# Reordering the prelude of a graph network kernel: edges loaded twice, a list made inside the scatter loop, and sixteen tiles taken up early

## The chip, the core and the metric

One core of a Trainium2 chip runs the whole kernel in one launch. The metric is the device time of one execution in microseconds (us). Engines are named as in the profile: PE (TensorE), PEld (its weight loads), DVE (VectorE), ACT (ScalarE), POOL (GpSimd) and SP (SyncE, which here only starts transfers).

## The reference

There are 6250 nodes of 256 features and 100,000 edges, sorted by destination. Two graph layers alternate with two mixtures of experts:

```python
edge_index = stack([src, dst])
x = x + L0_gnn(layernorm(x), edge_index, edge_weight)    # weighted, normed, self loops, two dense layers
x = x + L0_ffn(layernorm(x))                             # 8 experts, 2 taken
x = x + L1_gnn(edge_index, layernorm(x), edge_type_8)    # 8 relations
x = x + L1_ffn(layernorm(x))                             # 6 experts of three layers, 2 taken

# inside L0_gnn: rows are edge_index[0] (src), cols are edge_index[1] (dst)
deg  = segment_sum(edge_weight with 1 for self loops, row)
norm = rsqrt(deg)[row] * edge_weight * rsqrt(deg)[col]
xw   = x @ W
h    = segment_sum(xw[col] * norm[:, None], row) + b
out  = relu(h @ W1 + b1) @ W2 + b2
```

Layer 1 takes `hx[edge_type, src]` for each edge and sums it over `dst`.

## The kernel before, in words

Nodes are worked on in 49 blocks (`NT`) of 128. Edges come in 782 tiles (`C_`) of 128, and are padded to 784 (`TN`). Layer 0 turns every edge's product row into a message, which is scattered to a place in memory (`msgs`) where all messages of one source block lie together. A later stage sums them with matmuls. The stages that concern the change are these.

**The edges and the first branch (0 to about 49 us).** `e_dst`, `e_src`, `e_edge_type` and `e_edge_weight` are loaded as 125 partitions of 800. DVE counts for blocks 1 to 21 how many destinations lie below each block (`eqd`, L178), and ACT does so for blocks 22 to 48 (`sgd`, L183, a Sign with a running sum). Both fill `ltd`. POOL and DVE build four-word records (`rec`), which go to memory as `edge_table` and are read back by tile as `Mn` (128 partitions, 7 groups of 128 edges). A branch at L217 asks whether the edges need sorting. They don't.

**Layer 1's list (about 49 to 94 us).** From `Mn` come the lanes, the transposed `srcT` and `ewT`, and `lane_rows` in memory. `tile_list` then derives from `ltd` which edge tiles each destination block needs (`steps`, `past`, `natq_i`). Seven indirect gathers on POOL (L389) bring the tiles' records as `M`, from which `dlocT` and `idxT` are made for layer 1. Then the pool `edges` (`loading`, right side of the memory) is closed, and the next pool, `keys`, takes its room.

**Statistics, weights, block counts (about 50 to 143 us).** x is loaded by pairs of tiles (`xa`, L537) for the layer norm's mean and variance, and W is multiplied with W1 (`ww`). DVE compares each source block with 49 numbers (`eq`, L594), PE counts the result (`pcnt`), and a chain of small operations with a scan (L614) gives every block its start.

**Places and x@W (about 143 to 243 us).** For each of the 49 blocks, PE makes the places (`ppos`, L652 and L653), which DVE copies under a mask (L654). Between them the generator `x_times_w` loads x a second time and takes a tile at a time: ACT norms it (`xn`, L551), PE transposes it (`pt_x`), ACT copies it (`xT`), PE multiplies it (`pxw`, L562), ACT copies the product (L563), and SP writes it to `xw`.

**Degrees (about 243 to 372 us).** 28 chunks, each with a one-hot tensor (`ohl`, L722) and three weighted ones (`we`, L730) from DVE for PE's `pdeg` (L737).

**Scaling and scatter (about 372 to 1427 us).** `xw` is read back as `acc`, and ACT scales the 49 tiles by the degree's root (L775). A branch at L870 chooses between near and far edges; all are near. Its branch `messages` takes 98 turns of eight edge tiles. SP loads the turn's lanes three turns ahead (`rowsn`). DVE makes a selection `sT` (L823) and copies the sources into the message (L833). PE picks the rows (`pxn`, L842), ACT scales them by the edge weight (L857), and POOL scatters them with one indirect transfer per edge tile (L860).

The program is written with pools of tiles and generators. A scheduler decides the order of instructions on each engine, so it can differ from the order of the text. Each engine then works its own queue in order.

Of the kernel before, what the change touches and what calls it, by code (L numbers as in the profile page):

```python
# [8 lines left out]
F32 = mybir.dt.float32  # L9
I32 = mybir.dt.int32  # L10
# [32 lines left out]
RW = 260  # L43
DCH = 28
# [12 lines left out]
def gnn_ffn_kernel(ctx: ExitStack, tc: tile.TileContext, a, out):  # L57
# [20 lines left out]
    gap = graph_a.enter_context(tc.tile_pool(name="graph_a", bufs=1))  # L78
    loading = ctx.enter_context(ExitStack())
# [11 lines left out]
    src = load_edges("src", I32)  # L91
    et = load_edges("edge_type_8", I32)
    ew = load_edges("edge_weight", F32)
# [62 lines left out]

    table = dram.tile([C_, 128 * 4], I32, name="edge_table")  # L160
    records = table.rearrange("c (e r) -> (c e) r", r=4)
    rec = sp.tile([EP, EC, 4], I32, name="rec")
    recf = rec.bitcast(F32)
    hi_i = sp.tile([EP, EC], I32, name="hi_i")
    nc.vector.tensor_scalar(hi_i, dst, 7, None, op0=OP.arith_shift_right)
    hi = sp.tile([EP, EC], BF16, name="hi")
    nc.vector.tensor_copy(hi, hi_i)


    ltd = sp.tile([EP, NT + 1], F32, name="ltd")  # L170
    nc.vector.memset(ltd[:, 0:1], 0.0)
    nc.vector.memset(ltd[:, NT:], float(EC))
    edge = sp.tile([128, NT], F32, name="edge")
    nc.vector.tensor_scalar(edge, lanes_i[:, :NT], -1.0, 0.5, op0=OP.mult, op1=OP.add)
    by_count = 22
    for b in range(1, by_count):
        eqd = sp.tile([EP, EC], BF16, name=f"eqd{b}", tag="eqd")
        nc.vector.tensor_scalar(  # L178
            eqd, hi, float(b), None, op0=OP.is_lt, op1=OP.add, accum_out=ltd[:, b : b + 1]
        )  # L180
    for b in range(by_count, NT):
        sgd = sp.tile([EP, EC], BF16, name=f"sgd{b}", tag="sgd")
        nc.scalar.activation(  # L183
            sgd, hi, AF.Sign, bias=edge[:EP, b : b + 1], accum_out=ltd[:, b : b + 1]
        )
    nc.vector.tensor_scalar(
        ltd[:, by_count:NT], ltd[:, by_count:NT], -0.5, float(EC // 2), op0=OP.mult, op1=OP.add
    )
    nc.gpsimd.tensor_copy(rec[:, :, 0], dst)
    nc.gpsimd.tensor_copy(rec[:, :, 1], src)  # L190
    nc.gpsimd.tensor_copy(recf[:, :, 2], ew)
    nc.vector.scalar_tensor_tensor(rec[:, :, 3], src, float(NR), et, op0=OP.mult, op1=OP.add)
    nc.sync.dma_start(records[:E].rearrange("(p c) r -> p (c r)", p=EP), rec)
    pad = sp.tile([C_ * 128 - E, 4], I32, name="pad")
    nc.vector.memset(pad, 0)
    nc.vector.memset(pad[:, 0:1], NP + 128)
    nc.sync.dma_start(records[E:], pad)

    falls = sp.tile([EP, 2], F32, name="falls")
    fall = sp.tile([EP, EC], BF16, name="fall")  # L200
    nc.vector.tensor_tensor(fall[:, : EC - 1], hi[:, 1:], hi[:, : EC - 1], OP.is_lt)
    nc.vector.tensor_reduce(falls[:, 0:1], fall[:, : EC - 1], axis=AX.X, op=OP.max)
    nhi_i = sp.tile([EP, 1], I32, name="nhi_i")
    nc.vector.tensor_scalar(nhi_i, dnext, 7, None, op0=OP.arith_shift_right)
    nhi = sp.tile([EP, 1], BF16, name="nhi")
    nc.vector.tensor_copy(nhi, nhi_i)
    nc.vector.tensor_tensor(falls[:, 1:2], nhi, hi[:, EC - 1 :], OP.is_lt)
    pfall = psum_sm("pfall")
    nc.tensor.matmul(pfall[:1, :2], ones[:EP, 0:1], falls, start=True, stop=True)
    nfall = sp.tile([1, 1], F32, name="nfall")  # L210
    nc.vector.tensor_reduce(nfall, pfall[:1, :2], axis=AX.X, op=OP.max)
    nfall_i = sp.tile([1, 1], I32, name="nfall_i")
    nc.vector.tensor_copy(nfall_i, nfall)
    unsorted = nc.values_load(
        nfall_i[0:1, 0:1], min_val=0, max_val=EP, skip_runtime_bounds_check_because="it is a count"
    )
    with tc.If(unsorted > 0):  # L217
        with tc.tile_pool(name="reorder", bufs=1) as rp:
            cntd = rp.tile([EP, NT], F32, name="cntd")
            nc.vector.tensor_sub(cntd, ltd[:, 1:], ltd[:, :NT])  # L220
            ptot = psum_sm("ptotd")
            nc.tensor.matmul(ptot[:EP, :NT], ones[:EP, :EP], cntd, start=True, stop=True)
            ppre = psum_sm("ppred")
            nc.tensor.matmul(ppre[:EP, :NT], before[:EP, :EP], cntd, start=True, stop=True)
            tot = rp.tile([EP, NT], F32, name="totd")
            nc.vector.tensor_copy(tot, ptot[:EP, :NT])
            base = rp.tile([EP, NT], F32, name="based")
            nc.vector.tensor_tensor_scan(base, ones[:EP, :NT], tot, -1.0, op0=OP.mult, op1=OP.add)
            nc.vector.tensor_sub(base, base, tot)
            nc.vector.tensor_add(base, base, ppre[:EP, :NT])  # L230
            pos = rp.tile([EP, EC], F32, name="posd")
            one = ones[:EP, 0:1].to_broadcast([EP, EC])
            eq = rp.tile([EP, EC], BF16, name="eqd2")
            run = rp.tile([EP, EC], F32, name="rund")
            for b in range(NT):
                nc.vector.tensor_scalar(eq, hi, float(b), None, op0=OP.is_equal)
                nc.vector.tensor_tensor_scan(run, one, eq, base[:, b : b + 1], op0=OP.mult, op1=OP.add)
                nc.vector.copy_predicated(pos, eq.bitcast(U16), run)
            pos_i = rp.tile([EP, EC], I32, name="posd_i")
            nc.vector.tensor_copy(pos_i, pos)  # L240
            for c in range(EC):
                ins = nc.gpsimd.indirect_dma_start(
                    out=records,
                    out_offset=bass.IndirectOffsetOnAxis(ap=pos_i[:, c : c + 1], axis=0),
                    in_=rec[:, c, :],
                    in_offset=None,
                )
                tc.declare_no_dep(ins.ins, group="reorder", reason="every edge has a place of its own")
                tc.add_to_no_dep_group("reorder", ins.ins)

    def tile_list(s, pool, e0, e1, turns):

        def col1(name, dt=F32):
            return pool.tile([NT, 1], dt, name=f"{name}{s}", tag=f"tl_{name}")

        some = col1("some")  # L260
        nc.vector.tensor_tensor(some, e1, e0, OP.is_gt)
        e0_i, e1_i = col1("e0", I32), col1("e1", I32)
        nc.vector.tensor_copy(e0_i, e0)
        nc.vector.tensor_scalar(e1_i, e1, 127.0, None, op0=OP.add)
        nc.vector.tensor_scalar(e0_i, e0_i, 7, None, op0=OP.arith_shift_right)
        nc.vector.tensor_scalar(e1_i, e1_i, 7, None, op0=OP.arith_shift_right)
        f, nt = col1("f"), col1("nt")
        nc.vector.tensor_copy(f, e0_i)
        nc.vector.tensor_sub(nt, e1_i, e0_i)
        nc.vector.tensor_mul(nt, nt, some)  # L270
        pt0 = psum_sm(f"pt0_{s}")
        nc.tensor.matmul(pt0[:NT, 0:1], before[:NT, :NT], nt, start=True, stop=True)
        tend, ahead = col1("tend"), col1("ahead")
        nc.vector.tensor_add(tend, pt0[:NT, 0:1], nt)
        nc.vector.tensor_sub(ahead, f, pt0[:NT, 0:1])
        psh = psum_sm(f"psh_{s}")
        nc.tensor.matmul(psh[:NT, 0:1], nextup[:NT, :NT], ahead, start=True, stop=True)
        steps = pool.tile([NT, 2], F32, name=f"steps{s}", tag="tl_steps")
        nc.vector.memset(steps, 1.0)
        nc.vector.tensor_copy(steps[:, 1:2], psh[:NT, 0:1])  # L280
        past = pool.tile([NT, turns], F32, name=f"past{s}", tag="t4")
        nc.vector.tensor_scalar(past, turn[:NT, :turns], tend, None, op0=OP.is_ge)
        return steps, past, tend

    Mn = sp.tile([128, QN, 128, 4], I32, name="Mn")
    nc.vector.memset(Mn[:, QN - 1], NP + 128)
    whole = (QN - 1) * 128
    nc.sync.dma_start(  # L290
        Mn[:, : QN - 1].rearrange("p q e r -> p q (e r)"), table[:whole].rearrange("(q p) x -> p q x", p=128)
    )
    nc.sync.dma_start(Mn[: C_ - whole, QN - 1].rearrange("p e r -> p (e r)"), table[whole:])
    Mnf = Mn.bitcast(F32)
    firstb_i = sp.tile([128, QN], I32, name="firstb_i")
    nc.vector.tensor_scalar(firstb_i, Mn[:, :, 0, 0], 7, None, op0=OP.arith_shift_right)
# [447 lines left out]
    for _ in xws:  # L744
        pass
# [916 lines left out]
```

## Time and profile before

| what | us |
|---|---|
| the three runs | 4180.68, 4183.84, 4184.01 |
| their median | 4183.84 |
| the profiled execution | 4184.38 |
| its span in the trace | 4182.6 |
| first message scatter starts | 400.7 |
| last message scatter | about 1427 |

The profile has one execution of the program. Its time is 1.8 us longer than the span of its records. Rows of groups give busy time and mean duration, and then the time that the engine stood idle ahead of them, with what ended that idle time. A row of a stretch of time gives the busy time of each engine in it.

### The profile page before, as it was taken

The page shows a single profiled execution, that of the slowest core. Times are in us where ns is not written, and L with a number is a line of the kernel's source. Part 1 is how long each engine was busy: PE and PEld are TensorE (multiplying, and loading weights), DVE is VectorE, ACT ScalarE, POOL GpSimd, SP SyncE. Part 2 cuts the span into 40 slices and gives each one's busy share as a digit, 9 for nine tenths or more (in the row PEclk, how much of TensorE's full clock was granted, in tenths as well). Part 3 has the DMA queues.
Part 4 walks back from the last instruction along what each step waited for, and adds up shares of the span by engine and source line. Part 5 has one row for each costly group of instructions (what it writes and reads, how often), then busy time and mean ns, then how long its engine had stood idle before and what let it go on. Part 6 is the DMA issues. An engine that isn't in the chain of part 4 may idle for free.

```text
span 4182.6 us, 53223 instructions
## 1 busy us (share of the span) xinstructions
PE 3478.2 (83%) x14645; PEld 2313.5 (55%) x14645; DVE 2083.1 (50%) x5720; ACT 1310.2 (31%) x2934; POOL 2261.2 (54%) x2440
## 2 busy tenths in 40 slices
PE   2887777777777568888969967998679999999999
PEld 1565656655656345555547733444356666666656
DVE  6686211111111146777853367664456666666652
ACT  3312333333333212333324434665012222222213
POOL 1001777777777524555550057333767777777750
PEclk8998999999999788999989988999689999999999
DMA  5514433333333434555643335445645555555540
GB/s 178 170 38 148 131 128 127 128 128 127 127 127 128 159 102 158 191 201 188 214 165 108 109 122 199 196 196 201 187 140 152 151 153 153 147 154 153 146 115 9
DMA packets 233067, 612.09 MB, mean 146 GB/s; under 512 B 41908, under 2 KB 126103, under 8 KB 212783
## 3 DMA queue, kind: packets, MB, share of 16 engines
q0 software_dynamic: 100624, 294.88, 22.7%
q1 hardware_dynamic: 112636, 290.21, 20.8%
q10 hardware_dynamic: 19488, 23.31, 1.6%
q8 instruction: 132, 2.16, 0.2%
q14 instruction: 187, 1.53, 0.1%
HBM read 371.49 MB, written 236.79 MB: 145 GB/s over the span
## 4 chain that ended last, share of the span: by engine, by line
PE 41%; DVE 12%; DMA 5%; issue 5%; POOL 2%; ACT 2%; DVEq 1%; ACTq 0%; SPq 0%; POOLq 0%
PE ph_e1a L475 6%; PE py1a L1007 6%; PE pa1a L928 6%; PE ph_e2a L475 5%; PE pa0e L901 4%; PE phx L1425 4%; DMA g0e<-msgs 3%; DVE acc L903 3%; PE pf L1344 2%; PE pf L1360 2%; DVE rest L1435 1%; DVE acc L932 1%; PE pt_fh L463 1%; DVE hx L1419 1%; PE pg2e L1094 1%
## 5 line engine op out<-in xcount | busy, mean ns | idle before, releaser
L860 POOL DMA_INDIRECT msgs<-msgn,at x782 | 787.4, 1007 | 550.3 <-DMA M<-edge_table,natq_i 313.6
L920 POOL DMA_INDIRECT g1a<-hx,idxT x830 | 828.6, 998 | 319.1 <-PE pa1a L928 142.5
L842 PE MATMUL pxn<-acc,sTn 128*128 x3128 | 792.2, 413 | 242.1 <-DVE sTn L823 215.3
L842 PEld LDWEIGHTS pxn<-acc,sTn 128*128 128x128 f32 x3128 | 613.9, 206 | 420.3 <-DVE sTn L823 282.2
L901 PE MATMUL pa0e<-g0e,m0e 128*128 128x256 f32 x1660 | 503.3, 436 | 157.5 <-DVE acc L903 71.8
L857 ACT ACTIVATE msgn<-pxn,ewT 128x256 f32<-128x256 f32 x782 | 370.1, 473 | 638.5 <-PE pxn L842 468.0
L932 DVE TENSOR_TENSOR acc<-acc,pa1a 128x256 f32 x830 | 346.7, 418 | 341.8 <-PE pa1a L928 309.8
L901 PEld LDWEIGHTS pa0e<-g0e,m0e 128*128 128x128 f32 x1660 | 293.0, 207 | 330.6 <-issue 128.5
L898 POOL TENSOR_SCALAR m0e<-minus,keye 128x128 f32<-128x128 f32 x414 | 259.5, 641 | 320.0 <-PE pa0e L901 275.7
L833 DVE COPY msgn<-srcT 128x32 f32<-128x32 f32 x98 | 17.5, 181 | 831.1 <-DMA msgs<-msgn,at 722.1
L928 PE MATMUL pa1a<-g1a,m1a 128*128 128x256 bf16 x2490 | 375.6, 283 | 51.6 <-DMA g1a<-hx,idxT 35.0
L928 PEld LDWEIGHTS <-m1a 128*128 128x128 bf16 x2490 | 244.0, 100 | 275.2 <-issue 192.3
L903 DVE TENSOR_TENSOR acc<-acc,pa0e 128x256 f32 x830 | 347.2, 418 | 92.7 <-PE pa0e L901 42.9
L1425 PE MATMUL phx<-wr,xT 128*128 128x512 f32 x784 | 368.5, 613 | 29.1 <-DVE rest L1435 21.6
L1007 PE MATMUL py1a<-w_L_ffn_expert_w,v2a 128*128 128x256 f32 x1176 | 286.6, 384 | 6.0 <-DVE acc L932 3.0
L475 PE MATMUL ph_e1a<-xT3a,w_L_ffn_expert_w 128*128 128x512 f32 (+2 forms) x672 | 287.9, 555 | 0.0
L475 PE MATMUL ph_e2a<-v1a,w_L_ffn_expert_w 128*128 128x512 f32 (+2 forms) x672 | 280.1, 542 | 2.1 <-DVE acc L932 1.3
L482 ACT ACTIVATE v1a<-ph_e1a,cols 128x512 f32<-128x512 f32 (+2 forms) x168 | 106.5, 634 | 538.8 <-PE ph_e1a L475 525.7
L1425 PEld LDWEIGHTS phx<-wr,xT 128*128 128x128 f32 x784 | 148.2, 197 | 188.5 <-issue 161.2
L1385 POOL DMA_INDIRECT y<-ys,ats x98 | 97.5, 995 | 277.5 <-issue 262.2
L1007 PEld LDWEIGHTS py1a<-w_L_ffn_expert_w,v2a 128*128 128x128 f32 x1176 | 208.8, 190 | 44.2 <-ACT v2a L482 10.3
L1008 DVE SCALAR_TENSOR_TENSOR X<-py1a,C1a,X 128x256 f32<-128x256 f32 x294 | 138.9, 480 | 112.3 <-PE py1a L1007 111.4
(646 smaller groups left out, 4373.2 us busy)
## 6 DMA issues: line engine op xcount, KB each, us to landing
g0e<-msgs SPq DMA_DIRECT2D x104, 1040.0 KB
hx<-hx SPq DMA_DIRECT2D x49, 1536.0 KB
rowsn<-lane_rows SPq DMA_DIRECT2D x98, 256.0 KB
fx<-xs SPq DMA_DIRECT2D x105, 128.0 KB
ys<-fy ACTq DMA_DIRECT2D x105, 128.0 KB
g1a<-hx,idxT POOLq DMA_INDIRECT x830, 3.1
msgs<-msgn,at POOLq DMA_INDIRECT x782, 2.4
msgs<-none ACTq DMA_DIRECT2D x10, 650.0 KB
```

The lines of the kernel that those rows point to most:

```text
L475: nc.tensor.matmul(ps[:, :ncols], w[:, k, f * 128 : (f + 1) * 128], xT[:, k, :ncols], start=(k == 0), stop=(k == 1),)
L842: nc.tensor.matmul(come, sT[:, k, j, :], acc[:, bass.ds(blocks[j] * D + k * D, D)], start=(k == 0), stop=(k == 1),)
L857: nc.scalar.activation(msg[:, j, :D], come, AF.Copy, scale=ewT[:, t0 + j : t0 + j + 1])
L860: ins = nc.gpsimd.indirect_dma_start(out=msgs, out_offset=bass.IndirectOffsetOnAxis(ap=at[:, t0 + j : t0 + j + 1], axis=0), in_=msg[:, j, ...
L898: nc.gpsimd.tensor_scalar(m[:, j], minus, key[:, j : j + 1], None, op0=OP.is_equal)
L901: nc.tensor.matmul(ps[:, :D], m[:, j, :], g[:, j, :D], start=True, stop=True)
L903: nc.vector.tensor_add(here, here, ps[:, :D])
L920: nc.gpsimd.indirect_dma_start(out=g, out_offset=None, in_=table, in_offset=bass.IndirectOffsetOnAxis(ap=idxT[:, t0 + j : t0 + j + 1], axi ...
L928: nc.tensor.matmul(ps[:, :D], m[:, j, :], g[:, k * D : (k + 1) * D], start=(k == 0), stop=(k == 2))
L932: nc.vector.tensor_add(here, here, ps[:, :D])
L1007: nc.tensor.matmul(ps[:, :D], hT[:, k, j : j + 128], w[:, k, :], start=(k == 0), stop=(k == 1))
L1425: nc.tensor.matmul(ps, xT[:, k, :], wr[:, k, r : r + 2, :].rearrange("p r o -> p (r o)"), start=(k == 0), stop=(k == 1),)
```

## The change

The changed kernel takes up the work ahead of the scatter in another order.

- The three edge arrays that are needed by tile are loaded from the inputs in that form too (`dst_n`, `src_n`, `ew_n`). `edge_table` is still written, now by POOL's queue, and is not read back as a whole unless the edges have to be sorted.
- The first 16 tiles of x are loaded on ACT's queue and stay in memory (`x1`). Their statistics and norms come before the first branch, and their products with `ww` before the pool `edges` is closed. The norms' root is taken on DVE by `inverse_root`, not with ACT's square root.
- All 48 counts of destinations are on ACT, and stand in the text ahead of the degrees. DVE's part of the counts is gone, save in the branch that sorts.
- Layer 1's list, and the block lists of layer 0's sums, are made by a generator `lists`. From the eleventh turn of the scatter loop on, each turn takes one step of it. The seven gathers take one buffer `M` in turn.
- The lanes are loaded two turns ahead, not three.
- The scaling of `acc` is split: odd tiles on DVE, even ones on ACT.

```diff
+X1 = 16
...
-    src = load_edges("src", I32)
-    et = load_edges("edge_type_8", I32)
-    ew = load_edges("edge_weight", F32)
+    def load_tiles(name, dt, fill):
+        t = sp.tile([128, QN, 128], dt, name=f"n_{name}")
+        nc.vector.memset(t[:, QN - 1], fill)
+        e0, e1 = (QN - 1) * 128 * 128, E // 128 * 128
+        nc.sync.dma_start(
+            t[:, : QN - 1], a[name][:e0].rearrange("(q p e) -> p q e", p=128, e=128)
+        )
...
+    dst_n = load_tiles("dst", I32, NP + 128)
+    src_n = load_tiles("src", I32, 0)
+    ew_n = load_tiles("edge_weight", F32, 0.0)
+    x1 = sp.tile([128, X1, D], F32, name="x1")
+    for t in range(0, X1, 4):
+        nc.scalar.dma_start(
+            x1[:, t : t + 4], a["x"][t * 128 : (t + 4) * 128].rearrange("(t p) d -> p t d", p=128)
+        )
...
+    src = load_edges("src", I32)
+    et = load_edges("edge_type_8", I32)
+    ew = load_edges("edge_weight", F32)
...
-    by_count = 22
-    for b in range(1, by_count):
-        eqd = sp.tile([EP, EC], BF16, name=f"eqd{b}", tag="eqd")
-        nc.vector.tensor_scalar(
-            eqd, hi, float(b), None, op0=OP.is_lt, op1=OP.add, accum_out=ltd[:, b : b + 1]
-        )
-    for b in range(by_count, NT):
-        sgd = sp.tile([EP, EC], BF16, name=f"sgd{b}", tag="sgd")
-        nc.scalar.activation(
-            sgd, hi, AF.Sign, bias=edge[:EP, b : b + 1], accum_out=ltd[:, b : b + 1]
-        )
...
-    nc.vector.scalar_tensor_tensor(rec[:, :, 3], src, float(NR), et, op0=OP.mult, op1=OP.add)
-    nc.sync.dma_start(records[:E].rearrange("(p c) r -> p (c r)", p=EP), rec)
+    row8 = sp.tile([EP, EC], I32, name="row8")
+    nc.gpsimd.tensor_scalar(row8, src, float(NR), None, op0=OP.mult)
+    nc.gpsimd.tensor_tensor(rec[:, :, 3], row8, et, OP.add)
+    nc.gpsimd.dma_start(records[:E].rearrange("(p c) r -> p (c r)", p=EP), rec)
...
+    for t in range(X1):
+        x_stats(t, x1[:, t])
+    x_norms(0, X1)
+    multiply_weights()
     unsorted = nc.values_load(
...
-    nc.sync.dma_start(
-        Mn[:, : QN - 1].rearrange("p q e r -> p q (e r)"), table[:whole].rearrange("(q p) x -> p q x", p=128)
-    )
...
-    nc.vector.tensor_scalar(real, Mn[:, :, :, 0], float(NP), None, op0=OP.is_lt)
+    nc.vector.tensor_scalar(real, dst_n, float(NP), None, op0=OP.is_lt)
...
-    nc.sync.dma_start(lane_rows.rearrange("(q p) e -> p q e", p=128), laneb)
+    nc.gpsimd.dma_start(lane_rows.rearrange("(q p) e -> p q e", p=128), laneb)
...
-    steps, past, tend = tile_list("d", sp, bounds[:, 0:1], bounds[:, 1:2], Q * 128)
...
-    M = sp.tile([128, Q, 128, 4], I32, name="M")
-    for q in range(Q):
-        nc.gpsimd.indirect_dma_start(
...
-    dlocT = to_edges("dlocT", ed, Q, lambda q: dloc[:, q], BF16)
-    idxT = to_edges("idxT", ed, Q, lambda q: idxf[:, q], I32)
+    xws1 = x_times_w([(t, 2) for t in range(0, X1, 2)], x1)
+    for _ in xws1:
+        pass
     loading.close()
...
+    pairs = [(t, min(2, NT - t)) for t in range(X1, NT, 2)]
+    for t, n in pairs:
+        x = x_tiles(t, n, "a")
+        for i in range(n):
+            x_stats(t + i, x[:, i])
+    x_norms(X1, NT)
+    xws = x_times_w(pairs)
...
+    for b in range(1, NT):
+        sgd = kp.tile([EP, EC], BF16, name=f"sgd{b}", tag="sgd")
+        nc.scalar.activation(sgd, hi, AF.Sign, bias=edge[:EP, b : b + 1], accum_out=ltd[:, b : b + 1])
...
-        nc.scalar.activation(here, here, AF.Copy, scale=dinv[:, t : t + 1])
+        if t % 2:
+            nc.vector.tensor_scalar(here, here, dinv[:, t : t + 1], None, op0=OP.mult)
+        else:
+            nc.scalar.activation(here, here, AF.Copy, scale=dinv[:, t : t + 1])
...
+    def lists(pool, tag):
...
+        for q in range(Q):
+            M = pool.tile([128, 128, 4], I32, name=f"M{tag}{q}", tag="M")
+            nc.gpsimd.indirect_dma_start(
+                out=M.rearrange("p e r -> p (e r)"),
+                out_offset=None,
+                in_=table,
+                in_offset=bass.IndirectOffsetOnAxis(ap=natq_i[:, q : q + 1], axis=0),
+            )
+            yield
+            both = pool.tile([128, 2, 128], F32, name=f"both{tag}{q}", tag="both")
+            nc.vector.tensor_scalar(both[:, 0], M[:, :, 0], first[:, q : q + 1], None, op0=OP.subtract)
+            nc.vector.tensor_copy(both[:, 1], M[:, :, 3])
+            yield
...
-        with tc.tile_pool(name=f"expand{tag}", bufs=3) as xp:
+        with tc.tile_pool(name=f"expand{tag}", bufs=2) as xp, tc.tile_pool(name=f"lists{tag}", bufs=1) as lp:
...
-            ahead = [lanes_of(t0) for t0 in (0, 8, 16)]
+            ahead = [lanes_of(t0) for t0 in (0, 8)]
+            later = lists(lp, tag)
...
-                if t0 + 24 < TN:
-                    ahead.append(lanes_of(t0 + 24))
+                if t0 + 16 < TN:
+                    ahead.append(lanes_of(t0 + 16))
+                if t0 >= 80:
+                    next(later, None)
```

## The prediction

> **What bounds the kernel now.** I read the page's slices first, then busy time by stage, then groups of instructions in the first 401 us, then branches and waits. The change reaches two places only: the prelude, up to the first message scatter at 400.7 us, and the scatter itself, up to about 1427 us. The other 2756 us keep their instructions, so I cost them at nothing.
>
> ```profile
> DVE  6686211111111146777853367664456666666652
> ACT  3312333333333212333324434665012222222213
> POOL 1001777777777524555550057333767777777750
> PEclk8998999999999788999989988999689999999999
> ...
> L860 POOL DMA_INDIRECT msgs<-msgn,at x782 | 787.4, 1007 | 550.3 <-DMA M<-edge_table,natq_i 313.6
> L833 DVE COPY msgn<-srcT 128x32 f32<-128x32 f32 x98 | 17.5, 181 | 831.1 <-DMA msgs<-msgn,at 722.1
> ```
>
> A digit is a 104.6 us slice. In the scatter (slices 5 to 13) POOL shows 7, DVE 1. POOL issues 782 scatters in (1427 - 400.7) = 1026 us, 1.31 us each, 1.007 of them busy. DVE idles 722 us there for message buffers. So POOL bounds the scatter, and small DVE, PE or ACT work is free there; POOL instructions are not.
>
> The prelude has no single bound. Busy time by stage:
>
> ```profile
> 0.00:50.00 50.00, 0.50 (x3) 0.27 (x3) 31.72 (x80) 29.75 (x55) 8.11 (x14) 1.00 0.29 103
> 50.00:100.00 50.00, 22.81 (x94) 15.14 (x95) 28.34 (x110) 10.10 (x21) 7.97 (x9) 0.63 0.76 259
> 100.00:143.00 43.00, 27.23 (x122) 15.25 (x122) 37.61 (x134) 6.54 (x15) 0.00 (x0) 0.78 0.36 101
> 143.00:243.00 100.00, 94.63 (x479) 65.71 (x478) 53.59 (x101) 52.81 (x136) 0.00 (x0) 0.97 0.56 175
> 243.00:372.00 129.00, 112.46 (x788) 92.50 (x786) 121.34 (x121) 0.37 (x1) 0.00 (x0) 0.95 0.01 4
> 372.00:401.00 29.00, 3.56 (x8) 2.87 (x9) 5.51 (x19) 20.58 (x51) 0.28 (x1) 0.53 0.97 311
> ```
>
> After the stretch and its length come PE, PEld, DVE, ACT, POOL, granted clock, DMA share, GB/s. To 50 us DVE and ACT count edges; to 143 everything waits in turn; to 243 PE is full (places and x@W); to 372 DVE is full (degrees) and ACT empty; to 401 ACT scales.
>
> ```profile
> L183 ACT ACTIVATE sgd<-hi,edge 125x800 bf16<-125x800 bf16 x27 | 26.0, 961 | 17.3 <-DVE edge L174 16.4
> L537 DVE BATCH_NORM_STATS2 st<-xa 128x6 f32<-128x256 f32 x49 | 19.1, 409 | 10.5 <-DMA xa<-in_x 10.4
> L594 DVE TENSOR_SCALAR eq<-hib 128x784 bf16<-128x784 bf16 x49 | 14.3, 350 | 0.0
> L654 DVE COPY_PREDICATED pos<-eq,ppos 128x392 f32<-128x392 uint16 x98 | 52.5, 587 | 44.4 <-PE ppos L653 44.3
> L551 ACT ACTIVATE xn<-xb,shift,ln_o 128x256 f32<-128x256 f32 x49 | 26.9, 601 | 2.9 <-DVE shift L543 2.9
> L775 ACT ACTIVATE acc<-acc,deg_o 128x256 f32<-128x256 f32 x49 | 19.9, 493 | 4.3 <-DMA acc<-xw 4.3
> ```
> ```profile
> 133.15 2.07 PE L562 MATMUL pxw<-ww,xT 128*128 128x256 f32 x4
> ...
> 149.26 1.03 PE L562 MATMUL pxw<-ww,xT 128*128 128x256 f32 x4
> ```
> ```profile
> L870 DVEq COMPARE_BRANCH  x1: 72/72/72, 375.1 to 375.1; - x1
> L870 SPq COMPARE_BRANCH  x1: 50/50/50, 385.3 to 385.3; - x1
> ```
>
> **The change part by part**, along the chain of stages.
>
> *To the first branch.* DVE passes L217 at 48.5 us in before, after waiting 11.5 us for ACT's 27 counts. Gone from DVE: 21 counts (20.6 + 1.7 us), that wait, and the record product (1.6). Added: statistics of 16 tiles, 16 x (0.39 + 0.17) = 9 us, and a dozen small operations, 2 to 3 us. DVE is then limited by arrival: edges twice (2.8 MB), x1 (2.1 MB). At the 259 GB/s of the second stretch 4.9 MB take 19 us, and land at about 25; statistics and norms end near 36 (30 to 42). POOL's own additions (row product and sum about 4 us beside copies of 2.0, 2.0, 1.6) end near 29, an estimate from those copies, ahead of it. x1's four issues take at most 6 us of ACT (five fillers took 7.3 later), which idles 16 us there; the nine tile loads share SP's queue with the later edge loads, and only POOL's copies wait for those; the table and lane writes now on POOL's queue meet a POOL idle until the scatter, and only gathers 600 us later read the table: nothing each. The table write (1.6 MB, 17.3 to 33.1 us in before, the read-back's end) is no longer waited for here. **-12.5** (-7 to -18.5). The Trainium skill, "DMA: Bandwidth & Descriptors", section "Issuing engines are not separate DMA queues", speaks against this part: transfers issued by different engines run on the same 16 DMA engines, so moving x1 to ACT's queue buys issue time, not bandwidth. The row shows a share of only 0.29 in the first 50 us, so there is room; by the rule with the 103 GB/s of that row, 4.9 MB would take 48 us and all this gain would be gone. I take 259, since the small figure is mostly idle.
>
> *Branch to the free edge pool.* In before, layer 1's list (seven gathers, landing 4.2 us each, its small chain, 62.6 to 93.9 us) holds the right-hand pool; the next stage starts at 93.6. In after the list is gone, but the pool holds x1, and the next stage waits for the last x1 tile to be normed. That is a new serial chain. srcT and ewT come about 6 us behind the branch as now (42), then eight pairs. Pair time warm: PE 2 x (0.60 transposes + 1.03 products) = 3.3, with hand-overs 3.6; cold 2 x (1.06 + 2.07) = 6.3 by the first line at 133 us. The Trainium skill, "TensorE: Matmul & The Clock Gate", section "Part 1: The HAM clock gate", says that an idle window of about 3.4 us halves the clock. The granted clock in this stretch is 0.63, so both happen. Warm, the last norm comes at 42 + 7.5 x 3.6 = 69; cold at 42 + 7.5 x 6.3 = 89. Because PE has continuous work here, I take 69 (64 to 80). The pool's free point moves from 93.6 to 69: -24.6, of which 12.5 are counted above, so **-12**. DVE meanwhile does the other 33 tiles' statistics (18.5 us), which fit the 33 us from branch to 69.
>
> *Equality and counts of blocks.* 93.6 to 127.1 in before, 33.5 us: 49 eq (14.3), statistics between, and waits for xa. With the statistics gone ahead, 14.3 + 3 = 17.2. **-16**.
>
> *To the first predicated copy.* 15.9 us in before (127.1 to 143.0). ACT's counts are now 48, at 0.96 + 0.19 less overlap = 1.087 each. The diff puts them beside the degrees, where ACT is empty; the schedule puts 15 of them, 16.3 us, ahead of ACT's copy of the block counts, on which scan and places wait. With the norms of the remaining tiles and three xn between, the copy comes 20.3 us into this step, then 8.5 us of scan chain: 28.8. **+13** (0 to +17; had the schedule followed the text it were 0).
>
> *Places and x@W.* 100.3 us in before, PE-bound at 4.07 per two blocks. In after 33 tiles remain and each two carry two counts: ACT 1.10 + 0.65 + 0.72 + 2.17 = 4.65, so ACT becomes the bound: 16.5 x 4.65 = 77, minus 9 already done in the gap before, plus the last 16 blocks at DVE's 1.07 = 17. 84 to 85. **-16** (-8 to -22).
>
> *Degrees.* DVE-bound, same instructions: 0. Cover for the counts if they ran here: 129 us of idle ACT.
>
> *Scaling and the branch.* 49 scales at 0.406 on ACT become 25 there and 24 on DVE; alone -2, because the last loaded piece lands no earlier than 394.1 on the old clock. But DVE, which passed L870 at 375.1 and had 6.3 us of jump hidden, now passes it behind the last piece, near 395.5; then message copies, first list operations (0.64) and the first sT (1.47). SP and POOL are already past. The first scatter comes 6 us later after the end of the degrees: **+6** (0 to +8).
>
> *Scatter.* Seven gathers on POOL at 1.28, an iota 0.2, and the second gather two scatters behind the first, into the same buffer: its landing and two DVE operations less two scatters leave a stall of 1.5. **+10.7** (+9 to +20). Hidden: about 35 small PE, 14 DVE and ACT operations, under DVE's 722 us of waiting; without this cover about 15 us. The lanes' loads, three ahead before and two now, land 5.9 us after issue and have two turns, 21 us.
>
> Sum: -12.5 - 12 - 16 + 13 - 16 + 6 + 10.7 = **-27**. Against the profiled execution's 4184.4 (span 4182.6) that is 4157; the median, 4183.8, is 0.5 lower, which I ignore.
>
> **The rivals.**
>
> A. *More than that.* The norms wait less and x1 arrives early (branch at 31, pool free at 62), the second gather doesn't stall and DVE's jump costs 2: -27 - 7 - 4 - 2 = -40: 4144. For it: ACT and DMA have idle room everywhere. Against: each step must go well.
>
> B. *Cold TensorE.* The pair chain runs at 6.3, the pool is free at 89 to 92: -27 + 22 = -5: 4179, no change that can be told. For it: PEclk 0.63 and the two product lines. Against: in this stretch PE idled behind DVE and gathers, which go.
>
> C. *Slower: the pool is held still longer.* x1's chain is the one thing that holds it now. If PE and ACT alternate without overlap on a cold clock, a pair takes 6.3 + 2.5 (ACT's 2 x (0.55 + 0.33 + 0.36)) = 8.8: free at 42 + 7.5 x 8.8 = 108, 39 later: +12: 4196. It decides from (8.4 + 27)/7.5 = 4.7 us beyond 3.6, so 8.3 a pair. For it: each tile goes ACT, PE, ACT, PE, ACT. Against: three xn buffers and two pairs of output let the tiles overlap, as they do after 149 us.
>
> D. *It doesn't do what it says*: the counts really hide under the degrees, none ahead of the copy: -40, which joins A; or they are all in front: 33 more x 1.087, of which the places stage gives back most: about -18, inside my range.
>
> **How the numbers follow.** About 0.2% (8.4 us) can be told from no change. Chances: forecast 0.60 (4146 to 4172), A and the good side of D 0.17, B 0.13, C 0.10. Range: 4137 (A and a little) to 4183 (B whole), leaving out most of C and the far end of A. Faster: 0.60 + 0.17 = 0.77, same 0.13, slower 0.10.
>
> **What would show it.** Right: the first branch on DVE near 36; products in x1's chain at 1.03 per tile; the first block equality near 69; ACT counts ahead of the copy; pair cycle 4.65; first scatter near 363; scatter stage 1037 us with seven gathers. Wrong: the first equality beyond 90 (B, C), a scatter stage beyond 1046, or any longer stage after it. Outside the first 1400 us there should be no difference over 3 us.

## The result

The changed kernel took 4165.88 us (median of 5 runs, 4165.19 to 4166.91), the kernel before 4183.84 in the same set. The ratio is 0.9956 (95% interval 0.9943 to 0.9969): 18 us faster, where 27 were forecast. The profiled span went from 4182.6 to 4164.9 us, 17.7 less. A second set on another chip gave 4171.28 against 4182.07, ratio 0.9969 (0.9959 to 0.9980), so the gain is 11 to 18 us by the two medians.

The slices of the changed kernel's page and its rows for the scatter and the message copies:

```profile
DVE  4596111111111146787853367664556666666652
ACT  2802433333333212333324434665012222222113
POOL 1002777777777525555550057333777777777750
...
L919 POOL DMA_INDIRECT msgs<-msgn,at x782 | 785.2, 1004 | 271.2 <-DMA msgs<-msgn,at 128.6
L892 DVE COPY msgn<-srcT 128x32 f32<-128x32 f32 x98 | 17.8, 184 | 825.8 <-DMA msgs<-msgn,at 730.9
```

DVE's first slice fell from 6 to 4, ACT's second rose from 3 to 8: that is where most of the counts went. The scatter reads as before, POOL at 7 and DVE waiting 731 us for message buffers. Busy time by stage, with the changed kernel's own boundaries (stretch and length, then PE, PEld, DVE, ACT, POOL, clock, DMA share, GB/s):

```profile
0.00:52.00 52.00, 7.35 (x31) 5.45 (x31) 19.09 (x91) 7.09 (x14) 13.77 (x20) 0.94 0.76 226
52.00:88.00 36.00, 24.99 (x113) 18.77 (x114) 17.75 (x67) 15.99 (x42) 0.99 (x1) 0.81 0.68 227
...
135.00:217.00 82.00, 74.48 (x375) 48.81 (x374) 50.81 (x101) 60.81 (x148) 0.00 (x0) 0.98 0.53 168
```

In the first 52 us every engine is mostly idle (DVE busy for 19 us, POOL 14, ACT 7), while the DMA share is 0.76; in the first 50 us of the kernel before it was 0.29. The places (135 to 217) are still PE's: 74.5 of 82.

The steps by the starts of the instructions that bound them, in us:

| step | before | after | difference | forecast |
|---|---|---|---|---|
| start to DVE's first branch | 48.5 | 51.6 | +3.1 | -12.5 |
| branch to the free edge pool (`srcT_i`) | 45.1 | 36.8 | -8.3 | -12 |
| to the last equality | 33.1 | 18.2 | -14.9 | -16 |
| to the first predicated copy | 16.3 | 28.2 | +11.9 | +13 |
| places, to the last copy | 99.7 | 81.5 | -18.2 | -16 |
| degrees | 128.6 | 128.6 | 0 | 0 |
| scaling, to the first scatter | 29.4 | 33.4 | +4.0 | +6 |
| first to last scatter | 1024.3 | 1032.0 | +7.7 | +10.7 |
| from there to the end of the span | 2757.6 | 2754.6 | -3.0 | 0 |
| sum | 4182.6 | 4164.9 | -17.7 | -27 |

The -3.0 of the last step can't be put down to the change. The changed kernel, profiled once more (last experiment), took 2758.6 us there.

One step went against its sign: the branch. What held DVE there stands in its timeline (start, duration, operation, and in brackets the idle time and its end):

```profile
25.22 0.17 DVE L383 SCALAR_TENSOR_TENSOR shift<-mv,rstd 128x16 f32<-128x16 f32 x1
38.89 0.75 DVE L378 BATCH_NORM_STATS2 st<-xa 128x6 f32<-128x256 f32 x2 [13.50 <-DMA xa<-in_x]
...
49.97 0.75 DVE L378 BATCH_NORM_STATS2 st<-xa 128x6 f32<-128x256 f32 x2 [9.26 <-DMA xa<-in_x]
```

The branch itself, from the instructions of its line (durations in ns, then first and last start in us):

```profile
L394 DVEq COMPARE_BRANCH  x1: 67/67/67, 51.6 to 51.6; - x1
```

The sixteen tiles' norms were done at 25.4 us, 10 us earlier than I estimated for the branch. But the schedule put eight statistics of *later* tiles (`xa`, tiles 16 to 23) and the two sums for `b_mlp` ahead of the branch, and the statistics waited 22.8 us for their loads. The wait of 11.5 us for ACT's counts was gone, and two of 13.5 and 9.3 us stood in its place. In most of the second one (40 to 49 us) the transfers of POOL's queue took most of the DMA engines' time (packets, MB, and the packets' time as a share of the 16 engines):

```profile
q0 software_dynamic: 140, 1.60, 74.4%
```

That is the write of `edge_table` (1.6 MB), issued by POOL at 38.8 us. The pair of tiles that DVE waited for was issued at 39.7.

### The profile page after: what moved, and what is told of

Its sections match the earlier page's. It is cut to its first block, busy times and chain, and to the rows that moved or that the text cites. A ratio compares the mean times of both kernels' runs of the same rounds, so it can differ in the third digit from the quotient of the medians.

```text
span 4164.9 us, 53190 instructions
## 1 busy us (share of the span) xinstructions
PE 3468.8 (83%) x14645; PEld 2306.4 (55%) x14645; DVE 2066.1 (50%) x5728; ACT 1314.8 (32%) x2954; POOL 2261.3 (54%) x2447
## 4 chain that ended last, share of the span: by engine, by line
PE 41%; DVE 14%; DMA 11%; issue 6%; POOL 3%; ACT 3%; DVEq 1%; SPq 0%; ACTq 0%; POOLq 0%
DMA msgs<-msgn,at 6%; PE ph_e1a L252 6%; PE py1a L1068 6%; PE pa1a L989 6%; PE ph_e2a L252 5%; PE pa0e L962 4%; PE pxn L901 3%; DMA g0e<-msgs 3%; DVE acc L964 3%; PE pf L1405 2%; DVE rest L1496 2%; PE pf L1421 2%; PE phx L1486 2%; POOL msgs L919 1%; DVE hx L1480 1%
## 5 line engine op out<-in xcount | busy, mean ns | idle before, releaser
L919 POOL DMA_INDIRECT msgs<-msgn,at x782 | 785.2, 1004 | 271.2 <-DMA msgs<-msgn,at 128.6
```

Of the source, the lines that this page charges most:

```text
L919: ins = nc.gpsimd.indirect_dma_start(out=msgs, out_offset=bass.IndirectOffsetOnAxis(ap=at[:, t0 + j : t0 + j + 1], axis=0), in_=msg[:, j, ...
```

## The experiments

All kernels below are the changed kernel with further edits. Their preludes can be compared step by step: the changed kernel itself, run again, had its first scatter at 379.5 us against 378.3. The scatter itself took 1172 to 1180 us on the chips of the first two sets, where the kernel before took 4519 and 4514 us, and 1031 to 1040 on the chip of the last. So whole times are compared only as ratios within a set, and the mechanisms by the trace.

**Fillers held back.** The ten filler writes to `msgs` (650 KB each) depend on the finished places (the last tiles' own writes get another source, `none1`):

```diff
-    for t in range(C_, TL, 5):
-        nc.scalar.dma_start(by_tile[:, t : t + 5, :], none)
...
+    nc.vector.tensor_scalar(none[:, 0, 0:1], at[:, 0:1], 0.0, None, op0=OP.mult)
+    for t in range(C_, TL, 5):
+        nc.scalar.dma_start(by_tile[:, t : t + 5, :], none)
```

> The changed kernel, with its ten filler writes (650 KB each, five of them at 16 to 39 us on ACT's queue) held back until the places are done, so that they fall under the degrees. Theory (the first branch is late because transfers share the bandwidth, and I left the fillers out of the 4.9 MB): 4 x 0.65 MB less at 260 GB/s is 10 us; the weights land near 28 instead of 37.5, DVE passes the first branch near 42 instead of 51.6, the first block equality comes near 80 instead of 93, the whole is 8 to 10 us faster than the changed kernel. Rival (the branch is late because six statistics of later tiles and two bias sums stand ahead of it on DVE, with loads that have two buffers): weights earlier, branch not before 48, whole within 3 us of the changed kernel.

Ratio to before 0.9947 (0.9923 to 0.9971), median 4496.81 us. Branch at 47.6, weights used at 33.9, edge pool free at 76.2, first equality at 79.3 (theory: 80), first scatter at 371.3, 7 us earlier. The branch moved 4 us, near the rival's 48; the pool moved 12, as the theory had it. So the transfers matter, but in the chain behind the branch (8 us) more than ahead of it (4 us). Five of the 12 us were lost again ahead of the first scatter: the step to the first predicated copy took 34.1 us instead of 28.2. Some products of the chain in the changed kernel, and two in this one:

```profile
...
73.14 1.99 PE L322 MATMUL pxw<-ww,xT 128*128 128x256 f32 x8 [0.49 <-ACT xT L242]
...
78.34 2.63 PE L322 MATMUL pxw<-ww,xT 128*128 128x256 f32 x8 [2.77 <-ACT xT L242]
...
83.12 3.59 PE L322 MATMUL pxw<-ww,xT 128*128 128x256 f32 x8 [1.30 <-ACT xT L242]
```
```profile
67.90 1.99 PE L322 MATMUL pxw<-ww,xT 128*128 128x256 f32 x8 [0.30 <-ACT xT L242]
...
70.63 1.99 PE L322 MATMUL pxw<-ww,xT 128*128 128x256 f32 x8 [0.30 <-ACT xT L242]
```

Without fillers a pair takes 2.73 us; with them 3.8 on average (seven pairs from 60.7 to 87.5 us). The waits of ACT in the changed kernel and in this one (20 to 95 us) say why:

```profile
ACT xw L323 <- DMA xw<-xw: 14.2, 6, 4.7
```
```profile
ACT xw L323 <- DMA xw<-xw: 1.8, 2, 1.6
```

ACT's copies of the products waited for earlier products to be written out, because `y` has two buffers: 9.5 us before the pool was free (the last 4.7 of the 14.2 came later), and without fillers 0.2. Four fillers were issued from ACT's queue in that very stretch (at 62.8, 69.1, 72.0 and 77.2 us). What they slowed can be followed in SP's queue, which starts the loads of later tiles as well as these writes; a row is merged from its first issue to the end of its last:

```profile
67.21 5.16 SPq L299 DMA_DIRECT2D xa<-in_x  x2
72.43 1.43 SPq L325 DMA_DIRECT2D xw<-xw  x1
73.97 3.67 SPq L299 DMA_DIRECT2D xa<-in_x  x2
77.73 0.42 SPq L325 DMA_DIRECT2D xw<-xw  x1
```

The products written from 72.43 and 77.73 us on had been ready at 69.9 and 72.8. From the third pair on, a write stood 2.5 to 4.9 us behind loads of `xa`, which wait for one of two buffers; without fillers 0 to 1.9 us. From its issue to the copy that waited for it, a write then took another 3.3 to 6.0 us. How much of the 8 us is the queue and how much the transfer, no run separates, since holding the fillers back shortens both. The rule of the Trainium skill that spoke against the change, in "DMA: Bandwidth & Descriptors", section "Issuing engines are not separate DMA queues" (all engines' transfers interleave on the same 16 DMA engines), fits what shows here, though not with x1, for which I weighed it: loads and writes issued by SP were slowed by writes issued by ACT.

Clock was lost too. Behind the idle time of 2.77 us the granted clock fell from 0.99 (60 to 80 us) to 0.50 (80 to 84 us), and the two groups of eight products behind it took 2.63 and 3.59 us instead of 1.99.

**Selection tile early.** `sel`, the stationary operand of the block counts, is made ahead of the equalities:

```diff
+    sel = kp.tile([128, 2 * NT - 1], BF16, name="sel")
+    nc.vector.memset(sel, 0.0)
+    nc.vector.memset(sel[:, NT - 1 : NT], 1.0)
     srcT_i = kp.tile([128, TN], I32, name="srcT_i", tag="t1")
```

> The changed kernel, with the selection tile for the block counts made ahead of the 49 equalities, not behind them. In the schedule 3 counts of destinations then stand ahead of the copy of the block counts, not 15. Theory (ACT has a fixed sum of work from 109 us to the end of the places, and bounds both): PE's block counts end near 108 instead of 125, the first predicated copy comes 10 to 13 us earlier, but the 12 counts moved behind it lengthen the places by as much; whole within 4 us of the changed kernel. Rival (the wait ahead of the copy was the loss, the places have room): 10 to 13 us faster.

Ratio 0.9948 (0.9929 to 0.9967), median 4495.59 us. First predicated copy at 124.0 instead of 134.8, first scatter at 366.7 instead of 378.3: 11.6 us. The rival is right and my theory is wrong: the places took 80.7 us although ACT was busy for 71.7 of the 81 us from 124 us on, where it had been busy for 61 of 82. The lines of PE's block counts in the changed kernel and of this one:

```profile
L543 PE MATMUL pcnt<-eq,sel x98: 329/329/531, 107.2 to 124.8; 128*49 128x392 bf16 x98
```
```profile
L543 PE MATMUL pcnt<-eq,sel x98: 329/329/531, 93.9 to 112.9; 128*49 128x392 bf16 x98
```

In the changed kernel PE began its 98 matmuls at 107.2 us, right behind the setting of `sel` at 107.0, and behind all 49 equalities. Here they begin at 93.9, beside them. The edit takes away more than this wait: 3 counts of destinations instead of 15 stand ahead of the copy of the block counts, which comes at 113.1 us instead of 126.6.

**Counts late.** All 48 counts of destinations depend on the finished places, and so run under the degrees:

```diff
     nc.vector.tensor_scalar(edge, lanes_i[:, :NT], -1.0, 0.5, op0=OP.mult, op1=OP.add)
+    zero = kp.tile([128, 1], F32, name="zero")
+    nc.vector.tensor_scalar(zero, at[:, 0:1], 0.0, None, op0=OP.mult)
+    nc.vector.tensor_scalar(edge, edge, zero, None, op0=OP.add)
```

> The changed kernel, with the 48 counts of destinations made to depend on the finished places, so that all run under the degrees. Theory (two waits end together ahead of the copy of the block counts: ACT's counts at 126.5 and PE's block counts at 125.1): the first predicated copy gains 1.3 us at most, the places become PE-bound at 4.07 per two blocks instead of ACT-bound at 4.65; whole 1 to 6 us faster than the changed kernel, degrees as long as before. Rival (the counts alone were the wait of 12 us that I predicted): 10 us or more faster.

Ratio 0.9969 (0.9956 to 0.9983), median 4502.79 us. First predicated copy at 134.1, first scatter at 377.1: a gain of 1.2 us, as the theory had it. Taking the counts away from where I had found them gains nearly nothing, because PE's block counts end at nearly the same time, 125.9 us here.

**Both.**

> Both of the last two edits. Theory: neither wait is left; the copy of the block counts comes near 108, the scan is then bound by DVE's own small operations, the first predicated copy comes near 121 instead of 134.8, the places take 84 us instead of 81.5 (PE-bound): whole 9 to 12 us faster than the changed kernel, more than the two edits alone together. Rival (the sum of work on PE bounds this stage): no more than the better of the two alone.

Ratio 0.9946 (0.9928 to 0.9965), median 4498.8 us. First predicated copy at 125.3, first scatter at 368.6. That is 9.7 us better than the changed kernel but no better than the early selection tile alone, so the rival is right. The busy time in the places of the kernel with the early tile, and then of this one:

```profile
124.00:205.00 81.00, 74.06 (x378) 48.51 (x377) 50.68 (x99) 71.74 (x169) 0.00 (x0) 1.00 0.55 175
```
```profile
125.00:206.00 81.00, 75.53 (x379) 49.47 (x378) 50.34 (x99) 35.03 (x91) 0.00 (x0) 0.98 0.55 175
```

ACT (the fourth figure behind the length) has half the work, the stage is as long, and PE has 74 to 76 us in each. PE bounds the places, with counts and without.

**All scales on ACT.** The split of the scaling is undone:

```diff
-        if t % 2:
-            nc.vector.tensor_scalar(here, here, dinv[:, t : t + 1], None, op0=OP.mult)
-        else:
+        if True:
             nc.scalar.activation(here, here, AF.Copy, scale=dinv[:, t : t + 1])
```

> The changed kernel, with all 49 scales of acc back on ACT. Theory (as in the prediction: DVE, which passed the second branch early and hid its jump of 6 us, now passes it behind the last scaled tile): from the first read of acc to the first scatter 29 to 30 us as in the kernel before, not 33.4; first scatter near 374 instead of 378.3; 4 us faster than the changed kernel. Rival (ACT's jump takes its place): within 1 us of the changed kernel's first scatter.

Ratio 0.9948 (0.9929 to 0.9967), median 4490.72 us. First scatter at 373.1, 29.1 us behind the end of the degrees, 4.3 less than in the changed kernel: the theory. DVE's first message copies in the changed kernel and in this one:

```profile
373.29 0.44 DVE L892 COPY msgn<-srcT 128x32 f32<-128x32 f32 x4 [5.84 <-issue]
```
```profile
353.92 0.44 DVE L890 COPY msgn<-srcT 128x32 f32<-128x32 f32 x4 [6.34 <-issue]
```

DVE loses about 6 us behind the branch both times. Without scales on DVE that is 19 us earlier, where nothing waits for it.

**Later tiles held.** The loads of the tiles from 16 on wait until DVE is past the first branch, and the product of the weights comes behind it:

```diff
+        if held:
+            nc.vector.memset(x[:, 0, 0:1], 0.0)
+            nc.vector.tensor_scalar(x[:, 0, 0:1], firstb[:, 0:1], 0.0, None, op0=OP.mult)
...
     x_norms(0, X1)
-    multiply_weights()
...
+    multiply_weights()
     xws1 = x_times_w([(t, 2) for t in range(0, X1, 2)], x1)
```

> The changed kernel, with the loads of the tiles from 16 on held until DVE is past the first branch, and the product of the weights put behind it in the text, so that no statistics or bias sums of theirs stand ahead of the branch. Theory (order: the branch waited for the loads of these tiles, three of them in two buffers): DVE passes the branch near 27 instead of 51.6, the pool of the edges is free near 71 instead of 88.4, first scatter 5 to 15 us earlier. Rival (transfers alone: 8.5 MB must come in before): the branch is early, but the weights land no earlier than 35, the statistics of the later tiles end as late as before or later, first scatter within 3 us of the changed kernel's.

Ratio 0.9952 (0.9934 to 0.9970), median 4491.05 us. The branch came at 26.3 us:

```profile
L396 DVEq COMPARE_BRANCH  x1: 67/67/67, 26.3 to 26.3; - x1
```

So order held the branch, with all fillers in place: the theory's first number is met, and the 36 us of my prediction were even too late. But the pool was free at 84.4, only 4 us earlier, and the first scatter came at 376.2. The weights were in at 38, as the rival had it, yet its reason is not the whole one, and the edit itself made part of the wait. PE now had the weights' product behind a sum that waits for DVE:

```profile
57.01 0.20 PE L495 MATMUL pfar<-far,ones 128*1 128x7 f32 x2 [7.78 <-DVE far L493]
57.13 2.08 PE L278 MATMUL pww<-w_L_gnn_W,wT 128*128 128x256 f32 x4
60.61 2.08 PE L278 MATMUL pww<-w_L_gnn_W,wT 128*128 128x256 f32 x4 [1.40 <-DVE nfar_f L497]
```

The chain of pairs could not begin before 63 us, later than in the changed kernel (60.7). This run leaves open what an early branch is worth; a later one shows it for the kernel with three gains.

**Four tiles at once**, with the early selection tile (`X1 = 4` for `X1 = 16`).

> The kernel with the early selection tile (first scatter 366.7), but with 4 tiles of x taken up at once, not 16. Both have about as many counts of destinations ahead of the block counts (4 and 3). Theory (a tile costs 1.9 us in the chain that holds the pool, and PE 1.63 in the places): the pool is free some 22 us earlier, the places are 19 to 20 us longer; first scatter within 5 us, so that taking up 16 tiles gains next to nothing. Rival (they are hidden work: PE and ACT idle in that stretch anyway): first scatter 12 us or more later.

Ratio 0.9977 (0.9967 to 0.9988), median 4505.13 us. The pool is free at 68.0, 21 us earlier than with 16 tiles, as the theory had it. But the places took 111.1 us instead of 80.7, 30 longer, and the first scatter came at 383.4, 16.6 later. So the rival is right: taking up twelve more tiles in the early stretch is worth 16.6 us, 1.4 a tile. Of the 30 us, PE's busy time makes 17 (91.0 us against 74.1). Another 12 are one wait:

```profile
PE pt_x L240 <- ACT xn L311: 12.4, 1, 12.4
```

Now 45 tiles had their statistics behind the branch, the last at 118 us, and their norms were done at 122, 12 behind the first predicated copy. The 1.4 us a tile have this wait in them.

**Fillers held back and selection tile early.**

> The changed kernel with the fillers held back and the selection tile early, the two edits that gained alone (first scatter 371.3 and 366.7 against 378.3). Theory: different stages, so the gains add: first scatter near 360, about 18 us faster than the changed kernel. Rival (the second takes up the first's gain): near 366.

Ratio 0.9923 (0.9906 to 0.9939), median 4483.62 us. First predicated copy at 111.9, 23 us earlier than in the changed kernel, but first scatter at 365.4: the places took 91.1 us. The rival is right for the prelude: the second gain took up most of the first. The busy time in the places, to be compared with the early tile alone (the row of 124 to 205 us above):

```profile
111.90:203.50 91.60, 82.12 (x391) 53.58 (x390) 51.35 (x100) 70.28 (x169) 0.00 (x0) 0.93 0.52 161
```

PE was busy for 8 us more, and the granted clock was 0.93 instead of 1.00. The norms of the later tiles were done at 110.7 us, one before the first copy, but this moved little work into the places: the products of 33 tiles and the transposes of 33 fall there, 32 and 29 with the early tile alone. At 1.4 us a tile (35.3 us of products for 32 tiles and 8.4 us of transposes for 28 in the changed kernel's places) that is an estimate of 2 us. The lower clock is the likely rest (0.07 of 91 us is 6); no run isolates it.

**The three gains together**, with all scales on ACT.

> The changed kernel with the three edits that gained: fillers held back, selection tile early, all scales of acc on ACT. Theory (the scaling is a stage of its own, so its 5 us add to the 365.4 of the other two): first scatter near 360, 0.4% faster than the changed kernel. Rival (ACT's jump takes the gain): near 365.

4151.28 us against 4182.07, ratio 0.9929 (0.9915 to 0.9942). First scatter at 358.9, 6.5 earlier than without the scales: the theory.

**Later tiles held, bias sums alone behind the branch.** On top of the three, the loads are held as above; only the sums for `b_mlp` go behind the branch (with a second load of W1):

```diff
+    def bias_sums():
+        w1 = load_w(xp0, "L0_gnn_W1", "w1")
         for f in range(2):
             ps = psum_sm(f"pbm{f}")
...
+    bias_sums()
     xws1 = x_times_w([(t, 2) for t in range(0, X1, 2)], x1)
```

> The last kernel, with the loads of the tiles from 16 on held until DVE is past the first branch, and only the two bias sums put behind it (the product of the weights stays ahead, unlike in the earlier kernel that held them, where PE took it up behind a wait for DVE at 57 us). Theory (the pair chain starts when DVE is past the branch and the weights are in, and runs at 2.7 us a pair): branch near 27, weights near 28, pool free at 60 to 65 instead of 75.3, first scatter 5 to 10 us ahead of the last kernel's. Rival (statistics of the later tiles, which now begin later, hold the norms, and PE's x@W then sets the end of the places): pool free early, first scatter within 3 us or later.

4144.15 us against 4182.07, ratio 0.9909 (0.9894 to 0.9924). Branch at 24.2, pool free at 64.0 (75.9 without), first scatter at 353.1, 5.9 earlier: the theory, although the weights came at 32.9, not 28. This is the fastest kernel of the study: 38 us less than before and 27 less than the changed kernel in the same set. Of the 12 us that the pool gained, half arrive at the first scatter; DVE's statistics of the later tiles now end at 96.7 and the first predicated copy comes at 104.7.

**Gathers twice.** On the kernel with the three gains, each gather of layer 1's list is issued twice into the same buffer:

```diff
+            for again in range(2):
+              M = pool.tile([128, 128, 4], I32, name=f"M{tag}{q}{again}", tag="M")
+              nc.gpsimd.indirect_dma_start(
```

> The kernel with the three edits, with each of the seven gathers of layer 1's list issued twice into the same buffer. Theory (a gather in the scatter costs POOL's issue, 1.28 us each, and nothing else): scatter 9 us longer than in the kernel with the three edits. Rival (each costs its landing too, 3.4 us, by a wait for the buffer): 24 us longer or more. Rival (gathers fall into waits for messages and are free): under 3 us.

4153.96 us, ratio 0.9937 (0.9922 to 0.9952). The scatter lasted 1039.7 us against 1031.2: 8.5 for seven more gathers, 1.2 each. The sum is the theory's; its make is not. POOL's waits in the scatter of this kernel have a line that the kernel with the three gains lacks:

```profile
POOL Mn L824 <- DMA Mn<-edge_table,natq_in: 8.4, 6, 1.8
```

The second gather of a pair waited for the first to land, 8.4 us in all, beside 7 x 0.98 of its own time. That makes 15; the rest came back in the scatters, whose busy time was 777.9 us here and 784.2 there. That sum lies between 774.6 and 787.4 in the kernels of this study, so it isn't shown that the gathers caused it. Seven gathers cost 8 to 15 us; that they are free, or cost a landing each (24), is excluded.

**The changed kernel again.**

> The changed kernel as it is, on the chip of these runs. Its prelude should repeat (first scatter 378 within 1 us), and its ratio to the kernel before lie near 0.9956; the other kernels' ratios of this set are read against it.

4171.28 us, ratio 0.9969 (0.9959 to 0.9980), first scatter at 379.5, scatter 1032.9. The prelude repeats to 1.2 us; the ratio lies above the first set's, with intervals that overlap. The profiled span is 6.1 us longer than in the first set, 4.0 of it behind the last scatter, where nothing was changed; the cause stays open.

## Why the prediction was right in the main, and where not

*Right in sign and nearly in size:* the equalities (-14.9 for -16), the places (-18.2 for -16), the degrees, the scaling (+4.0 for +6) and the scatter (+7.7 for +10.7). The wait behind the split scaling is shown by undoing it. Doubling the gathers puts the price of seven between 8 and 15 us.

*The step that failed: "To the first branch", -12.5 forecast, +3.1 measured.* It missed by 15.6 us, more than the whole forecast did. The main term that was missing is order. I ended the stage with the norms of the sixteen tiles, and did not follow DVE's queue on to the branch: eight statistics of later tiles stood there, with loads in two buffers, and two sums that need the weights. Taking both away put the branch at 24 to 26 us, in one kernel with all fillers in place. No run takes away the statistics alone; PE ended the products for the sums at 43.5 us in the changed kernel, so the sums alone would have held the branch to about then (an estimate from that trace). The smaller term is traffic. x1 came in time: the norms were done at 25.4 us. But I had summed 4.9 MB of edges and x1, and 11.8 MB (226 GB/s for 52 us) moved before the branch. Left out were five fillers (3.3 MB), the weights (0.5), four pairs of x (1.0) and the write of `edge_table` (1.6), which I had put at nothing. The fillers' share of the late branch is 4 us; what the table's write cost stays open, since every kernel here has it. The bandwidth that I chose, 259 GB/s, was right (251 GB/s in the first 25 us).

*The second step, the pool (-8.3 for -12),* began later by 15.6 us for that reason. Its pair time of 3.6 us met 3.8, but by two errors that cancelled. I counted the transposes twice: the 0.60 us are four of them, those of two tiles, and without fillers a pair took 2.73. And I left out the wait for written products, which lengthened it again. Rival B's price for a cold clock was not reached: in the changed kernel the chain's stretch had a granted clock of 0.81, without fillers 1.00. The Trainium skill's rule of the clock gate, in "TensorE: Matmul & The Clock Gate", section "Part 1: The HAM clock gate", names an idle window of about 3.4 us. Here the clock fell after a gap of 2.77 us, so a shorter gap was enough, and the measurement decides.

*A sign of being wrong came true.* I had named a first equality beyond 90 us as the mark of B or C, and it came at 93.0. Neither was the reason, with a clock of 0.81 in that stretch and 3.8 us a pair: the late branch was. That the sum of all steps still fell into the forecast's span is in part luck: the places, the scaling, the scatter and the stretch behind it came out 10 us better than forecast.

*Right size, half the reason: "To the first predicated copy".* I put +13 down to 15 counts on ACT. They were there, and the copy of the block counts came behind them at 126.6. But PE's block counts ended only at 125, so without the counts the step lost 1.3 us of its length and no more. The operand that PE waited for, `sel`, was set ahead of the equalities in the kernel before (94.8 us) and behind them in the changed one (107.0). In the text its lines did not move; the statistics of the later tiles moved ahead of them, which is the likely reason. Of two waits that end together, only the later one shows at the engine that waits for both. The early selection tile took 11 us off the step; in its trace both are gone.

*Wrong bound: the places.* "ACT becomes the bound" at 4.65 per two blocks was wrong: the stage is as long with ACT at 71 us or at 35, and PE is busy for 74 to 76 of 81. That the size fitted was chance.

*The other rivals.* A (more than forecast) did not come about, but its parts were there to be had: the kernel with four edits is 27 us faster than the changed one. C (the pool held longer than before) was not reached: its chain started late but ran faster than its 8.3 us a pair, and the pool was free at 88.4 us against 93.6. Of D, neither half came about: 15 of the 48 counts stood ahead of the copy.

## What to carry to other kernels

When a stage is costed up to a branch or a stage's end, follow each engine's queue to that instruction: work of later stages that the scheduler put ahead of it counts, with the loads that it waits for. When loads are moved to the start, sum all traffic of that stretch, the writes that nobody waits for too: they cost through the queues and buffers of others. And take a wait away only after asking what ends next to it; two waits that ended within 2 us hid each other here.

## What was not expected of the hardware

Fillers that nothing waits for cost 12 us up to the free pool: 4 ahead of the branch, and 8 in a chain of ACT and PE that reads nothing of them, through loads and writes in SP's queue and two output buffers (9.5 us of ACT's waits for written products with them, 0.2 without). And behind a branch DVE stood idle: 5.4 to 6.5 us at the second branch in every kernel here, and at the first one 1.2 us in the kernel before, 3.3 in the changed one and 6.7 where the branch came at 24 us. What sets that time, no run shows.
